# Attention over a 64x64 image: second key tiles in one-pass products, and a second chain of accumulating transfers for the denominators

## The chip, the cores and the metric

The kernel runs on one core of one Trainium2 chip, with its five engines: TensorE (PE in the profile), VectorE (DVE), ScalarE (ACT), GpSimd (POOL) and SyncE (SP), and its 16 DMA engines. The metric is the device time of one execution in microseconds, the median of several runs.

## The reference

Four images of 64x64 pixels with 256 channels pass through two layers. The first is attention over all 4096 pixels of an image, with queries and keys of 32 channels:

```python
q = x @ Wq + bq
k = x @ Wk + bk
v = x @ Wv + bv
energy = jnp.einsum('bnd,bmd->bnm', q, k)
attn = jax.nn.softmax(energy, axis=-1)
x_out = jnp.einsum('bnm,bmc->bnc', attn, v)
out = gamma * x_out.reshape(B, H, W, Cin) + inputs
```

The second layer is a 3x3 depthwise convolution to 768 channels, a product to 512, gelu, a product back to 256, added to its input, and then attention of each pixel to its 3x3 neighbours, added again. All is in float32.

## The kernel before, in words

**Slots.** An image is worked on in eight blocks of 512 query pixels, which makes 32 slots (slot s is block s % 8 of image s // 8). In a slot the 4096 keys pass in 16 half groups of two key tiles of 128, one at each of 16 points. The exponentials p of a half group are a tile of 128 keys by 2 x 512 queries. The convolution layer follows some slots behind: its pieces (hidden_part at L721, update L778, guide L874, local_values L941, scores L982, local_product L1075 and others) are jobs dealt out to the points of later slots, and its taps on VectorE (L608, L614) are dealt out by the list `share`, one number for each point.

**A point.** Program order is queue order on each engine, and at point n it is: loads on SP (keys ka and values v, a group of two half groups ahead); for a half group of IN_PARTS the high part of p(n+1) on ScalarE (high_part, L389); energy (L379 on TensorE, exponential L384 on ScalarE) for half group n+2; the send of p(n+1) where it is one of BY_DMA (L429, L431); the loads of forms of v (load_forms) for n+3; the jobs; the product of half group n (L403 or L415); add_up of n+1 on VectorE; the taps. Two PSUM banks hold one energy tile e, so the next energy waits for the exponential before. p has three buffers.

**Products.** A plain half group is four float32 matmuls (two key tiles, two halves of the channels; L403); each stands in the profile as two instructions of 128x512, so eight a half group. A half group of IN_PARTS (the even ones from 2 to 14) is written as three products in the one-pass type float32r: high of p with a mixed form of v, then low and gap of p with two other forms of v, 12 instructions (L415) into two pairs of accumulators, which finish adds up. Its price elsewhere: high on ScalarE, low (pl, L444) and gap (pg, L449) on VectorE, and the loads of the forms. Slots from 1 to 30 except 2 do so (in_two_sums); the others are plain throughout.

**Denominators.** den of a slot is the sum of its 16 p over the half groups. VectorE adds the even ones and 1 and 15 (L447). The odd ones from 3 to 13 go by DMA: GpSimd issues transfers of p into the tile sent, of which the first writes and the rest accumulate. At the end of add_up for 15, VectorE adds sent (L455) and folds the two halves (L456); partial_sums transposes and reduces (L474, L475) the denominators and the local sums; finish multiplies the parts by a matrix on TensorE (dps, L493), takes reciprocals (L496) and forms the output.

**Projections.** Slot 0 and the last slot of each image (7, 15, 23) compute queries, keys and values of the next image (project_qk, project_v, L317 to L355). project_v writes v of each pair of key tiles to DRAM: plain ones to packed_v, and the three forms of those in IN_PARTS to packed_f, from staging tiles of the tag "vs" with four buffers. The stores of the forms are issued by GpSimd.

**Slot 0 and 1.** In slot 0 weights are loaded and prepared: wup1 of the hidden layer at point 1, turn_weights at points 6 to 11. In slot 1 GpSimd prepares wmix (L653), between the sends.

Of the kernel before, what the change touches and what calls it, by code (L numbers as in the profile page):

```python
# [52 lines left out]
BY_DMA = (3, 5, 7, 9, 11, 13)  # L53
# [6 lines left out]
def attention_then_perception_kernel(  # L60
# [37 lines left out]
    def unshifted():  # L98
# [113 lines left out]
        packed_f = tc.dram_tile([P, NSLOT * 2, 3, 2 * C], F32, name="packed_f")  # L212
# [4 lines left out]
        def in_parts(s, G, half):  # L217
            return in_two_sums(s) and 2 * G + half in IN_PARTS

# [77 lines left out]
        def load_values(s, G):  # L297
            values[s, G] = tile_of([P, TPB, C], "v", f"v_{s}_{G}", 2)
            to = values[s, G].rearrange("p t c -> p (t c)")
            at = 2 * block(s, G)  # L300
            if not any(in_parts(s, G, half) for half in range(2)):
                nc.sync.dma_start(out=to, in_=packed_v[:, bass.ds(at * 2 * C, TPB * C)])
                return
            for half in range(2):
                if in_parts(s, G, half):
                    of = packed_f[:, at + half, 0]
                else:
                    of = packed_v[:, bass.ts(at + half, 2 * C)]
                nc.sync.dma_start(out=to[:, bass.ts(half, 2 * C)], in_=of)

        def load_forms(s, G, half):
# [3 lines left out]
                in_=packed_f[:, 2 * block(s, G) + half, 1:3],  # L315
# [5 lines left out]
        def project_v(s, pair, tag="m"):  # L321
# [10 lines left out]
            split = 2 * (s % NBLK) + pair in IN_PARTS  # L332
            if not split or s < NBLK or s >= NSLOT - NBLK:
# [10 lines left out]
                )  # L344
            if split:
                low, high = (fresh(f"v{n}_{s}_{pair}") for n in "lh")
                nc.scalar.copy(low, of)
                nc.scalar.activation(high.bitcast(F32R), of, AF.Identity, scale=BELOW)
                nc.vector.tensor_tensor(low, low, high, ALU.subtract)
                gap = fresh(f"vg_{s}_{pair}")  # L350
                nc.vector.scalar_tensor_tensor(gap, low, -SPLIT, high, ALU.mult, ALU.add)
                nc.vector.tensor_scalar(low, low, SPLIT, None, ALU.mult)
                for i, part in enumerate((high, low, gap)):
                    nc.gpsimd.dma_start(
                        out=packed_f[:, 2 * s + pair, i], in_=part.rearrange("p t c -> p (t c)")  # L355
                    )

        def projections(s):
            pair = [lambda: project_qk(s)] if s % 2 == 0 else []
            order = sorted(range(2), key=lambda n: 2 * (s % NBLK) + n in IN_PARTS)  # L360
            return [lambda n=n: project_v(s, n) for n in order] + pair
# [29 lines left out]

        def product(s, G, half):
# [7 lines left out]
            if not in_parts(s, G, half):  # L400
                for i in range(2):
                    for c in range(CH):
# [3 lines left out]
                        )  # L406
                return
# [14 lines left out]
        def by_dma(s, n):  # L422
            return 0 < s < NSLOT - 1 and n in BY_DMA

        def send(s, n):
            p = weights[s, n // 2, n % 2]
            if n == BY_DMA[0]:
                sent[s] = tile_of([P, 2, NB], "sent", f"sent_{s}")
                nc.gpsimd.dma_start(out=sent[s], in_=p)  # L429
            else:  # L430
                nc.gpsimd.dma_start(out=sent[s], in_=p, accum_op=ALU.add)  # L431

        def add_up(s, G, half):

            if by_dma(s, 2 * G + half):
                return
            p = weights[s, G, half]
            if G == 0 and half == 0:
                sums[s] = tile_of([P, 2, NB], "den", f"den_{s}")
                return  # L440
            if in_parts(s, G, half):
                high = highs[s, G, half]
                low, gap = (tile_of([P, 2, NB], f"p{n}", f"p{n}_{s}_{G}_{half}") for n in "lg")
                nc.vector.tensor_tensor(low.bitcast(F32R), p, high, ALU.subtract)  # L444
            den = sums[s]
            before = weights[s, 0, 0] if (G, half) == (0, 1) else den
            nc.vector.tensor_tensor(den, before, p, ALU.add)  # L447
# [5 lines left out]
            if G == NG - 1 and half == 1:  # L453
                if s in sent:
# [1283 lines left out]
```

## Time and profile before

| | before |
|---|---|
| median of 3 runs | 3292.66 us (3291.38 to 3293.06) |
| profiled execution, its own time | 3292.32 us |
| its span, first to last instruction | 3290.5 us |
| mean granted TensorE clock | 0.998 |
| busy: PE, DVE, ACT, POOL | 3263.0, 2728.5, 1349.2, 619.9 us |
| DMA: moved, mean rate | 505.29 MB, 154 GB/s |
| DMA queues, share of 16 engines | q1 (hardware) 35.6%, q0 (issued by GpSimd) 15.5% |

Where slot 12 stands in the span: from about 1028.9 to 1124.9 us, 96.0 us, like most slots. In this stretch PE is busy 96.00, DVE 84.45, ACT 40.59 and POOL 18.33 us, and the DMA share is 0.52. Slots 7, 15 and 23 take about 132 us.

How to read the lines. A line of a group has engine, operation, tiles out<-in, shape and count, then busy us and mean ns of one, then the idle time of the engine just before and what ended it. A line of a timeline has the start in us, the duration in us, engine, line of the code, operation, tiles, and in brackets the idle time before and its releaser; several alike in a row are one line with a count. The durations of matmuls include pipelining, so they overlap: what one costs is the distance from start to start. "Chain" is the work that ended last, followed back from the last instruction, as shares of the span.

### The profile page before, as it was taken

The page shows a single profiled execution, that of the slowest core. Times are in us where ns is not written, and L with a number is a line of the kernel's source. Part 1 is how long each engine was busy: PE and PEld are TensorE (multiplying, and loading weights), DVE is VectorE, ACT ScalarE, POOL GpSimd, SP SyncE. Part 2 cuts the span into 40 slices and gives each one's busy share as a digit, 9 for nine tenths or more (in the row PEclk, how much of TensorE's full clock was granted, in tenths as well). Part 3 has the DMA queues.
Part 4 walks back from the last instruction along what each step waited for, and adds up shares of the span by engine and source line. Part 5 has one row for each costly group of instructions (what it writes and reads, how often), then busy time and mean ns, then how long its engine had stood idle before and what let it go on. Part 6 is the DMA issues. An engine that isn't in the chain of part 4 may idle for free.

```text
span 3290.5 us, 35859 instructions
## 1 busy us (share of the span) xinstructions
PE 3263.0 (99%) x11986; PEld 2170.3 (66%) x11986; DVE 2728.5 (83%) x4093; ACT 1349.2 (41%) x1647; POOL 619.9 (19%) x807
## 2 busy tenths in 40 slices
PE   9999999999999999999999999999999999999998
PEld 5556667666666666676666666666666666666655
DVE  4678888878888888887888888887788888888894
ACT  3334444444444444444444444444444444444331
POOL 2201111121222221122112222211221122222021
PEclk9999999999999999999999999999999999999999
DMA  6655555575545554558554455546755544555100
GB/s 212 211 165 142 149 149 146 163 227 175 147 141 155 164 154 143 153 165 246 146 153 145 145 155 156 163 141 183 236 160 145 152 147 144 155 157 154 48 25 27
DMA packets 272831, 505.29 MB, mean 154 GB/s; under 512 B 95152, under 2 KB 96192, under 8 KB 272512
## 3 DMA queue, kind: packets, MB, share of 16 engines
q1 hardware_dynamic: 231632, 370.15, 35.6%
q0 software_dynamic: 33328, 119.33, 15.5%
q10 hardware_dynamic: 7680, 13.44, 1.1%
q8 instruction: 99, 1.62, 0.2%
q14 instruction: 92, 0.75, 0.1%
HBM read 346.92 MB, written 60.69 MB: 124 GB/s over the span
## 4 chain that ended last, share of the span: by engine, by line
PE 96%; DVE 1%; issue 1%; ACT 1%; DMA 1%; POOL 0%; SPq 0%; ACTq 0%; DVEq 0%; POOLq 0%
PE acc L403 32%; PE acc L415 17%; PE e L379 7%; PE dx L778 6%; PE hid_bc L721 5%; PE hid_gf L721 5%; PE hid_de L721 5%; PE lv L941 3%; PE g L874 3%; PE v L326 3%; PE lo L1075 3%; PE s L982 3%; PE hid_a L721 2%; DVE perc L608 1%; PE qk L260 1%; PE hid L753 1%
## 5 line engine op out<-in xcount | busy, mean ns | idle before, releaser
L403 PE MATMUL acc<-p,v 128*128 128x512 f32 x2472 | 1113.8, 593 | 0.2 <-ACT v L340 0.2
L608 DVE SCALAR_TENSOR_TENSOR perc<-xp,wb,perc 128x526 f32<-128x526 f32 (+1 forms) x1356 | 964.1, 771 | 1.4 <-ACT perc L604 1.3
L384 ACT ACTIVATE p<-e 128x1024 f32<-128x1024 f32 x512 | 524.2, 1024 | 1004.6 <-PE e L379 925.7
L403 PEld LDWEIGHTS acc<-p,v 128*128 128x128 f32 x2472 | 466.5, 190 | 486.7 <-issue 472.1
L379 PE MATMUL e<-qa,ka 128*128 128x512 f32 x1024 | 426.8, 498 | 7.6 <-DMA ka<-packed 4.3
L431 POOL DMA_DIRECT2D sent<-p x150 | 129.5, 864 | 1337.5 <-ACT p L384 1328.5
L447 DVE TENSOR_TENSOR den<-den,p 128x1024 f32<-128x1024 f32 x268 | 340.7, 1271 | 9.3 <-ACT p L384 9.1
L444 DVE TENSOR_TENSOR pl<-p,ph 128x1024 fp32r<-128x1024 f32 x203 | 248.3, 1223 | 66.4 <-ACT ph L389 66.2
L389 ACT ACTIVATE ph<-p 128x1024 fp32r<-128x1024 f32 x203 | 214.4, 1056 | 198.4 <-PE acc L415 124.2
L379 PEld LDWEIGHTS e<-qa,ka 128*128 128x128 f32 x1024 | 189.8, 189 | 155.9 <-issue 132.3
L415 PE MATMUL acc<-ph,v 128*128 128x512 f32 x812 | 264.7, 447 | 0.0
L449 DVE SCALAR_TENSOR_TENSOR pg<-pl,ph 128x1024 fp32r<-128x1024 f32 x203 | 257.9, 1271 | 0.0
L778 PE MATMUL dx<-hid,wup 128*128 128x512 f32 x512 | 229.8, 592 | 0.0
L415 PE MATMUL acc<-pl,vf 128*128 128x512 f32 x812 | 223.0, 396 | 0.0
L415 PE MATMUL acc<-pg,vf 128*128 128x512 f32 x812 | 219.1, 391 | 1.0 <-DVE pg L449 1.0
L1030 POOL TENSOR_TENSOR lsum<-lsum,lp 128x99 f32<-128x99 f32 (+1 forms) x179 | 197.3, 1109 | 11.7
L1007 POOL TENSOR_TENSOR lp<-lp,near 128x396 f32<-128x396 f32 x60 | 109.2, 1821 | 396.5 <-ACT lp L1002 396.5
L415 PEld LDWEIGHTS acc<-ph,v 128*128 128x128 f32 x812 | 148.2, 189 | 51.2 <-issue 23.0
L415 PEld LDWEIGHTS acc<-pl,vf 128*128 128x128 f32 x812 | 152.8, 188 | 37.1
L415 PEld LDWEIGHTS acc<-pg,vf 128*128 128x128 f32 x812 | 152.5, 188 | 37.4 <-DVE pg L449 1.5
L744 ACT ACTIVATE hid<-hid,bup 128x512 f32<-128x512 f32 x120 | 80.1, 715 | 215.4 <-DVE hid L728 215.4
L614 DVE TENSOR_TENSOR perc<-perc 128x262 f32<-128x262 f32 x360 | 155.8, 447 | 8.1
(206 smaller groups left out, 4021.5 us busy)
## 6 DMA issues: line engine op xcount, KB each, us to landing
vf<-packed_f SPq DMA_DIRECT2D x203, 512.0 KB, 3.8
sent<-p POOLq DMA_DIRECT2D x180, 512.0 KB, 5.2
ka<-packed SPq DMA_DIRECT2D x1016, 64.0 KB, 2.9
v<-packed_f SPq DMA_DIRECT2D x203, 256.0 KB, 2.7
v<-packed_v SPq DMA_DIRECT2D x203, 256.0 KB, 2.9
v<-packed_v SPq DMA_DIRECT2D x45, 512.0 KB, 3.4
xp<-in_x SPq DMA_DIRECT2D x30, 528.0 KB, 6.2
xc<-in_x SPq DMA_DIRECT2D x56, 256.0 KB, 4.7
```

Of the source, the lines that this page charges most:

```text
L379: nc.tensor.matmul(e[:, i, :], lhsT=keys[s, G][:, bass.ts(2 * half + i, P)].bitcast(F32R), rhs=queries[s].bitcast(F32R), start=True, stop= ...
L384: nc.scalar.activation(p, e, AF.Exp)
L389: nc.scalar.activation(high.bitcast(F32R), weights[s, G, half], AF.Identity, scale=BELOW)
L403: nc.tensor.matmul(accs[s][c], lhsT=v[:, i, bass.ts(c, P)], rhs=p[:, i, :], start=(first and i == 0), stop=(last and i == 1),)
L415: nc.tensor.matmul(accs[s][to + c], lhsT=w[:, i, bass.ts(c, P)].bitcast(F32R), rhs=x[:, i, :].bitcast(F32R), start=(to > 0 and n == 0 and ...
L444: nc.vector.tensor_tensor(low.bitcast(F32R), p, high, ALU.subtract)
L447: nc.vector.tensor_tensor(den, before, p, ALU.add)
L449: nc.vector.scalar_tensor_tensor(gap.bitcast(F32R), low, -SPLIT, high, ALU.mult, ALU.add)
L608: nc.vector.scalar_tensor_tensor(acc, win, wt, acc, ALU.mult, ALU.add)
L721: nc.tensor.matmul(ps[:, n * C : (n + 1) * C], lhsT=w(j), rhs=rows_of(mixes[s, j][:, kind, :]), start=(j == 0), stop=(j == MULT - 1),)
L778: nc.tensor.matmul(ps, lhsT=wup2[:, d, bass.ts(c, P)], rhs=hids[s][:, d, :], start=(d == 0), stop=(d == NHC - 1),)
L1030: nc.gpsimd.tensor_tensor(to, to, near_ws[block, half][:, t_, of, :], ALU.add)
```

## The change

In 26 slots (those in two sums, except the last block of each image) the six odd half groups 3 to 13 are no longer plain throughout: tile 0 keeps its two float32 matmuls (four instructions) and tile 1 is written as three one-pass products, six matmuls (six instructions). For this each of them gets a load of two forms (load_one, 256 KB), a high part on ScalarE (high_one), and low and gap on VectorE, all in the four buffers of "vs". In the same slots the denominators of half groups 4, 6, 8, 10 and 12 go by a second chain of accumulating transfers, in a buffer of the tag "xc", and VectorE adds two sent sums at the end.

The layout in DRAM follows: packed_h has v as the first product needs it (one load of 512 KB where there were two of 256), packed_f has the two other forms, packed_o those of single tiles. project_v makes the forms for single tiles too, and stores plain values a second time into packed_h. The pairs of a block are always projected in the order 1, 0. The list share deals the same 54 taps out otherwise. The load of wup1 in slot 0 goes from point 1 to point 4, and turn_weights from points 6 to 11 to points 8 to 13.

```diff
@@ -50,7 +50,8 @@
 IN_PARTS = (2, 4, 6, 8, 10, 12, 14)
-BY_DMA = (3, 5, 7, 9, 11, 13)
+ONE_IN_PARTS = (3, 5, 7, 9, 11, 13)
+BY_DMA = (ONE_IN_PARTS, (4, 6, 8, 10, 12))
@@ -209,13 +210,18 @@
         packed_v = tc.dram_tile([P, NSLOT * TPB * C], F32, name="packed_v")
-        packed_f = tc.dram_tile([P, NSLOT * 2, 3, 2 * C], F32, name="packed_f")
+        packed_h = tc.dram_tile([P, NSLOT, TPB * C], F32, name="packed_h")
+        packed_f = tc.dram_tile([P, NSLOT, 2, 2 * C], F32, name="packed_f")
+        packed_o = tc.dram_tile([P, NSLOT, 2, C], F32, name="packed_o")
...
             return in_two_sums(s) and 2 * G + half in IN_PARTS
+
+        def one_in_parts(s, n):
+            return in_two_sums(s) and s % NBLK < NBLK - 1 and n in ONE_IN_PARTS
@@ -297,22 +303,27 @@
             to = values[s, G].rearrange("p t c -> p (t c)")
-            at = 2 * block(s, G)
-            if not any(in_parts(s, G, half) for half in range(2)):
-                nc.sync.dma_start(out=to, in_=packed_v[:, bass.ds(at * 2 * C, TPB * C)])
-                return
-            for half in range(2):
-                if in_parts(s, G, half):
-                    of = packed_f[:, at + half, 0]
-                else:
-                    of = packed_v[:, bass.ts(at + half, 2 * C)]
-                nc.sync.dma_start(out=to[:, bass.ts(half, 2 * C)], in_=of)
+            at = block(s, G)
+            if not in_two_sums(s):
+                nc.sync.dma_start(out=to, in_=packed_v[:, bass.ts(at, TPB * C)])
+            elif s % NBLK < NBLK - 1:
+                nc.sync.dma_start(out=to, in_=packed_h[:, at])
+            else:
+                nc.sync.dma_start(out=to[:, : 2 * C], in_=packed_h[:, at, : 2 * C])
+                nc.sync.dma_start(out=to[:, 2 * C :], in_=packed_v[:, bass.ts(2 * at + 1, 2 * C)])
...
                 out=forms[s, G, half].rearrange("p (f t) c -> p f (t c)", f=2),
-                in_=packed_f[:, 2 * block(s, G) + half, 1:3],
+                in_=packed_f[:, block(s, G)],
+            )
+
+        def load_one(s, n):
+            forms[s, n] = tile_of([P, NB], "vs", f"vo_{s}_{n}", 4)
+            nc.sync.dma_start(
+                out=forms[s, n].rearrange("p (f c) -> p f c", c=C),
+                in_=packed_o[:, block(s, n // 2)],
             )
@@ -329,7 +340,9 @@
             of = ps.rearrange("p (t c) -> p t c", c=C)
-            split = 2 * (s % NBLK) + pair in IN_PARTS
+            n = 2 * (s % NBLK) + pair
+            split, one = n in IN_PARTS, n in ONE_IN_PARTS
+            h = packed_h[:, s, bass.ts(pair, 2 * C)].rearrange("p (t c) -> p t c", c=C)
             if not split or s < NBLK or s >= NSLOT - NBLK:
@@ -342,23 +355,30 @@
                 )
+                if not split:
+                    tiles = slice(0, 1 if one else 2)
+                    nc.gpsimd.dma_start(out=h[:, tiles], in_=v[:, tiles])
             if split:
-                low, high = (fresh(f"v{n}_{s}_{pair}") for n in "lh")
-                nc.scalar.copy(low, of)
-                nc.scalar.activation(high.bitcast(F32R), of, AF.Identity, scale=BELOW)
-                nc.vector.tensor_tensor(low, low, high, ALU.subtract)
-                gap = fresh(f"vg_{s}_{pair}")
-                nc.vector.scalar_tensor_tensor(gap, low, -SPLIT, high, ALU.mult, ALU.add)
-                nc.vector.tensor_scalar(low, low, SPLIT, None, ALU.mult)
-                for i, part in enumerate((high, low, gap)):
-                    nc.gpsimd.dma_start(
-                        out=packed_f[:, 2 * s + pair, i], in_=part.rearrange("p t c -> p (t c)")
-                    )
+                low, high, gap = (fresh(f"v{n}_{s}_{pair}") for n in "lhg")
+                to = h, packed_f[:, s, 0], packed_f[:, s, 1]
+            elif one:
+                both, gap = (fresh(f"v{n}_{s}_{pair}") for n in ("lh", "g"))
+                low, high, gap, of = both[:, 0:1], both[:, 1:2], gap[:, 0:1], of[:, 1:2]
+                to = h[:, 1:2], packed_o[:, s, 0], packed_o[:, s, 1]
+            else:
+                return
+            nc.scalar.copy(low, of)
+            nc.scalar.activation(high.bitcast(F32R), of, AF.Identity, scale=BELOW)
+            nc.vector.tensor_tensor(low, low, high, ALU.subtract)
+            nc.vector.scalar_tensor_tensor(gap, low, -SPLIT, high, ALU.mult, ALU.add)
+            nc.vector.tensor_scalar(low, low, SPLIT, None, ALU.mult)
+            nc.gpsimd.dma_start(out=to[0], in_=high)
+            for at, part in zip(to[1:], (low, gap)):
+                nc.gpsimd.dma_start(out=at, in_=part.rearrange("p t c -> p (t c)"))
...
             pair = [lambda: project_qk(s)] if s % 2 == 0 else []
-            order = sorted(range(2), key=lambda n: 2 * (s % NBLK) + n in IN_PARTS)
-            return [lambda n=n: project_v(s, n) for n in order] + pair
+            return [lambda: project_v(s, 1), lambda: project_v(s, 0)] + pair
@@ -389,6 +409,12 @@
+        def high_one(s, n):
+            high = tile_of([P, NB], "vs", f"oh_{s}_{n}", 4)
+            p = weights[s, n // 2, n % 2]
+            nc.scalar.activation(high.bitcast(F32R), p[:, 1, :], AF.Identity, scale=BELOW)
+            highs[s, n] = high
+
         def product(s, G, half):
@@ -398,12 +424,24 @@
             if not in_parts(s, G, half):
-                for i in range(2):
+                one = one_in_parts(s, 2 * G + half)
+                for i in range(1 if one else 2):
                     for c in range(CH):
...
                         )
+                if one:
+                    at = s, 2 * G + half
+                    f = forms.pop(at)
+                    for w, to, x in (
+                        (v[:, 1], 0, highs[at]), (f[:, :C], 0, lows[at]), (f[:, C:], CH, gaps[at])
+                    ):
+                        for c in range(CH):
+                            nc.tensor.matmul(
+                                accs[s][to + c], lhsT=w[:, bass.ts(c, P)].bitcast(F32R),
+                                rhs=x.bitcast(F32R), start=False, stop=False,
+                            )
                 return
@@ -420,39 +458,54 @@
         def by_dma(s, n):
-            return 0 < s < NSLOT - 1 and n in BY_DMA
+            if n in BY_DMA[1]:
+                return one_in_parts(s, ONE_IN_PARTS[0])
+            return 0 < s < NSLOT - 1 and n in BY_DMA[0]
...
             p = weights[s, n // 2, n % 2]
-            if n == BY_DMA[0]:
-                sent[s] = tile_of([P, 2, NB], "sent", f"sent_{s}")
-                nc.gpsimd.dma_start(out=sent[s], in_=p)
+            even = 1 - n % 2
+            if n == BY_DMA[even][0]:
+                tag, bufs = ("xc", 2) if even else ("sent", 1)
+                sent[s, even] = tile_of([P, 2, NB], tag, f"sent_{s}_{even}", bufs)
+                nc.gpsimd.dma_start(out=sent[s, even], in_=p)
             else:
-                nc.gpsimd.dma_start(out=sent[s], in_=p, accum_op=ALU.add)
+                nc.gpsimd.dma_start(out=sent[s, even], in_=p, accum_op=ALU.add)
...
-            if by_dma(s, 2 * G + half):
-                return
+            n = 2 * G + half
+            if one_in_parts(s, n):
+                low, gap = (tile_of([P, NB], "vs", f"o{x}_{s}_{n}", 4) for x in "lg")
+                high = highs[s, n]
+                nc.vector.tensor_tensor(
+                    low.bitcast(F32R), weights[s, G, half][:, 1, :], high, ALU.subtract
+                )
+                nc.vector.scalar_tensor_tensor(
+                    gap.bitcast(F32R), low, -SPLIT, high, ALU.mult, ALU.add
+                )
+                lows[s, n], gaps[s, n] = low, gap
             p = weights[s, G, half]
...
                 return
+            den = sums[s]
+            before = weights[s, 0, 0] if (G, half) == (0, 1) else den
             if in_parts(s, G, half):
                 high = highs[s, G, half]
-                low, gap = (tile_of([P, 2, NB], f"p{n}", f"p{n}_{s}_{G}_{half}") for n in "lg")
+                low, gap = (tile_of([P, 2, NB], f"p{x}", f"p{x}_{s}_{G}_{half}") for x in "lg")
                 nc.vector.tensor_tensor(low.bitcast(F32R), p, high, ALU.subtract)
-            den = sums[s]
-            before = weights[s, 0, 0] if (G, half) == (0, 1) else den
-            nc.vector.tensor_tensor(den, before, p, ALU.add)
+            if not by_dma(s, n):
+                nc.vector.tensor_tensor(den, before, p, ALU.add)
             if in_parts(s, G, half):
...
             if G == NG - 1 and half == 1:
-                if s in sent:
-                    nc.vector.tensor_tensor(den, den, sent.pop(s), ALU.add)
+                for even in range(2):
+                    if (s, even) in sent:
+                        nc.vector.tensor_tensor(den, den, sent.pop((s, even)), ALU.add)
                 nc.vector.tensor_tensor(den[:, 0, :], den[:, 0, :], den[:, 1, :], ALU.add)
@@ -1161,7 +1214,7 @@
-            share = [2, 4, 8, 6, 4, 1, 7, 3, 6, 3, 4, 2, 2, 1, 1, 0]
+            share = [1, 5, 8, 6, 5, 2, 7, 4, 6, 3, 4, 2, 1, 0, 0, 0]
             if slot == NSLOT - 1:
@@ -1187,6 +1240,8 @@
                 after = slot + (G + 1) // NG, (G + 1) % NG
+                if one_in_parts(slot, point + 1):
+                    load_one(slot, point + 1)
                 if half == 0:
@@ -1198,6 +1253,8 @@
                     high_part(*behind)
+                if one_in_parts(slot, point + 1):
+                    high_one(slot, point + 1)
                 if after[0] < NSLOT:
@@ -1233,8 +1290,6 @@
                     wperc, bperc = wb[:, :, :, :TAPS], wb[:, :, :, TAPS]
-                    wup1 = loaded(w_up1, "wup1", queue=nc.gpsimd)
-                    bup1 = loaded(b_up1, "bup1", queue=nc.gpsimd)
                     gam = loaded(gamma.partition_broadcast(P), "gam", [P, 1])
@@ -1245,8 +1300,11 @@
                     clear_tap(point - MULT)
-                if slot == 0 and 2 * MULT <= point < 4 * MULT:
-                    turn_weights(*divmod(point - 2 * MULT, 2))
+                if slot == 0 and point == NG // 2:
+                    wup1 = loaded(w_up1, "wup1", queue=nc.gpsimd)
+                    bup1 = loaded(b_up1, "bup1", queue=nc.gpsimd)
+                if slot == 0 and NG <= point < NG + 2 * MULT:
+                    turn_weights(*divmod(point - NG, 2))
                 if slot == 0 and point == NG:
```

## The prediction

> **What bounds the kernel now.** I read the page from the top: busy shares, then the chain of work that ended last, then the costliest groups.
>
> ```profile
> PE 3263.0 (99%) x11986; PEld 2170.3 (66%) x11986; DVE 2728.5 (83%) x4093; ACT 1349.2 (41%) x1647; POOL 619.9 (19%) x807
> PE 96%; DVE 1%; issue 1%; ACT 1%; DMA 1%; POOL 0%; SPq 0%; ACTq 0%; DVEq 0%; POOLq 0%
> L403 PE MATMUL acc<-p,v 128*128 128x512 f32 x2472 | 1113.8, 593 | 0.2 <-ACT v L340 0.2
> L415 PE MATMUL acc<-pl,vf 128*128 128x512 f32 x812 | 223.0, 396 | 0.0
> L447 DVE TENSOR_TENSOR den<-den,p 128x1024 f32<-128x1024 f32 x268 | 340.7, 1271 | 9.3 <-ACT p L384 9.1
> L431 POOL DMA_DIRECT2D sent<-p x150 | 129.5, 864 | 1337.5 <-ACT p L384 1328.5
> ```
>
> TensorE is the bound: it is busy 99% and makes 96% of the chain. Its whole idle time, by the list of waits, is some 17 us. So PE time taken away shows one for one, as long as nothing else becomes late. VectorE, at 83%, is the next.
>
> The mean durations overlap (matmuls are pipelined), so prices must be start to start. The timeline of TensorE in slot 12 gives them:
>
> ```profile
> 1056.10 3.60 PE L403 MATMUL acc<-p,v 128*128 128x512 f32 x8
> 1059.13 1.02 PE L379 MATMUL e<-qa,ka 128*128 128x512 f32 x2
> 1059.99 1.46 PE L721 MATMUL hid_a<-perc,wup 128*128 128x256 f32 x6
> ...
> 1131.12 1.10 PE L415 MATMUL acc<-pl,vf 128*128 128x512 f32 x4
> 1132.05 1.07 PE L415 MATMUL acc<-pg,vf 128*128 128x512 f32 x4
> 1132.96 0.61 PE L379 MATMUL e<-qa,ka 128*128 128x512 f32 x2
> 1133.42 3.59 PE L403 MATMUL acc<-p,v 128*128 128x512 f32 x8
> 1136.85 0.30 PE L493 MATMUL dps<-parts,fold 128*128 128x32 f32 x2
> ```
>
> Eight f32 instructions take 1133.42 to 1136.85, 3.43 us, so 0.429 each. Eight one-pass ones take 1131.12 to 1132.96, 1.84 us, so 0.230 each; over all I use 0.232. The first three lines test a change of form: 1056.10 to 1059.99 is 3.89 us, and 8 x 0.429 + 2 x 0.230 is 3.89. Passing from f32 to one-pass costs nothing beyond the two.
>
> **What the Trainium skill says.** TensorE: Matmul & The Clock Gate, section Back-to-back issue gap, gives 512/2.4 + 2.5 ns, about 216 ns, for an isolated 512-column matmul. The trace has 0.230 us for a one-pass instruction, 7% above, and 0.429 for an f32 one, twice 0.215. The same page, section HAM oscillation, says that PE idle gaps over about 3.4 us slow the clock afterwards. The trace has one such gap:
>
> ```profile
> 39.08 1.19 PE L379 MATMUL e<-qa,ka 128*128 128x512 f32 x2 [4.27 <-DMA ka<-packed]
> 40.07 5.39 PE L403 MATMUL acc<-p,v 128*128 128x512 f32 x8
> ```
>
> Eight matmuls took 5.39 us there and 3.59 elsewhere: a long stall costs some 2 us on top of itself. DMA: Bandwidth & Descriptors, section Anatomy of one DMA, puts a transfer issued by GpSimd at 2.0 us plus bytes/436e3. For 512 KB that is 3.2 us. The first, plain transfer of slot 12 landed in 3.06, but the accumulating ones have a median of 5.2, and I use that.
>
> **The change, part by part.**
>
> *Products.* 26 slots (1, 3 to 6, 8 to 14, 16 to 22, 24 to 30) have six mixed half groups, 156 in all. Each drops four f32 instructions (4 x 0.429 = 1.716) and adds six one-pass ones (6 x 0.232 = 1.392). That is -0.324 us each and **-50.5 us** in all, 1.94 us of a slot's 96.0. L403 should fall from x2472 to x1848.
>
> *VectorE per slot.* Low and gap of each mixed half group are twelve 128x512 operations, some 0.65 us each (the add over 512 columns, L456, is 0.67 from start to start). Five L447 adds go, at 1.14 each. One more add of the sent sum is 1.44. Together 7.8 - 5.7 + 1.44 = +3.5. The taps are the same 54, only dealt out otherwise. A steady slot has 84.45 us of VectorE in 96.0; it would have some 88 in 94.1, 93%. That still fits; what matters is where it falls. The end of a slot is tightest:
>
> ```profile
> 1124.88 1.22 DVE L444 TENSOR_TENSOR pl<-p,ph 128x1024 fp32r<-128x1024 f32 x1 [1.81 <-ACT ph L389]
> 1128.86 0.59 DVE L614 TENSOR_TENSOR perc<-perc 128x262 f32<-128x262 f32 x1
> 1130.81 1.49 DVE L455 TENSOR_TENSOR den<-den,sent 128x1024 f32<-128x1024 f32 x1
> 1133.00 0.47 DVE L614 TENSOR_TENSOR perc<-perc 128x262 f32<-128x262 f32 x1
> 1135.53 0.69 DVE L475 TENSOR_REDUCE parts<-turned 128x16 f32<-128x512 f32 x1
> ```
>
> VectorE runs without a gap from 1124.88 to 1136.22, and PE needs the parts at 1136.85 (dps): 0.63 us to spare. After the change this stretch gains 1.44 (second sent) and loses the two L614 (0.51 + 0.39, moved to earlier points), while PE comes 0.32 earlier. So 0.63 - 0.54 - 0.32 is -0.23; with the signal, PE waits about 0.3 us, 0 to 0.8. Behind dps stand the next energies, so this delays everything. Over 26 slots **+8 us** (0 to 21). Ahead of it the 1.81 us of idle at 1124.88 take up low and gap of point 13 and the 1.0 us by which PE comes earlier in points 9 to 13.
>
> *ScalarE.* Six 128x512 copies a slot, about 0.62 each (half of L389's 1056 ns and a little): 40.6 to some 44 us of 94. Hidden; were it not, 3.7 us a slot.
>
> *Second chain.* POOL issues five more sends a slot, 0.864 us each, 18.3 to 22.6 us. Buffers of p turn over by three: the exponential of n+3 waits for the landing of send n. In a steady slot that is three points, some 18 us, against 0.9 + 5.2. It costs nothing there, and still nothing at 10 us of landing.
>
> *Slot 1* is the exception. Its points are short, and POOL does the turning of weights (wmix) before it can send. The timelines of POOL and ScalarE:
>
> ```profile
> 157.49 0.92 POOL L431 DMA_DIRECT2D sent<-p  x1
> 167.45 0.89 POOL L431 DMA_DIRECT2D sent<-p  x1 [9.04 <-DMA sent<-p]
> ```
> ```profile
> 158.54 1.02 ACT L384 ACTIVATE p<-e 128x1024 f32<-128x1024 f32 x1 [0.57 <-PE e L379]
> 162.48 1.02 ACT L384 ACTIVATE p<-e 128x1024 f32<-128x1024 f32 x1 [2.92 <-PE e L379]
> 166.98 1.03 ACT L384 ACTIVATE p<-e 128x1024 f32<-128x1024 f32 x1 [2.38 <-DMA sent<-p]
> ```
>
> The send at 157.49, of half group 11, took 9.4 us to land, and the last exponential waited for it. Now the send of half group 10 stands there first, behind wmix too, and the exponential of 13 (158.54) needs its landing, some 8 us later. The next energies (161.37) wait for that exponential, since e has one buffer; 1.8 us are to spare. So PE stalls 6.2 us and loses 2 by the clock: **+8 us** once (3 to 12).
>
> *Loads.* +66 MB of sends and some 39 MB of loads on 505 MB; the DMA share of a steady slot rises from 0.52 to some 0.65. load_one stands on SP's queue a point ahead, waiting for the product two before: 3 us of landing against 6 us. Hidden.
>
> *Projections.* In slots 7, 15 and 23 (132 us each) every pair that was one plain form becomes three forms or a plain one with a second store. POOL's stores go from 21 to 48 an image, some 0.55 us each. The four buffers "vs" now wait for these stores: ScalarE's copies stand in its queue ahead of the exponentials, and wait. Mostly that is below 1 us and covered. At the seventh block POOL's sum of the local weights (L1030, 1.1 us an operation) stands ahead of the stores, and the exponential comes some 3 us late. I take 3.5 us a slot, **+10 us** for three (3 to 30). The profile before shows the like at a smaller size: PE waited for the copy vh three times, 2.5 us in all.
>
> *Slot 0.* The load of wup1 (1.5 MB, 9.3 us) goes from point 1 to point 4, away from the ka load that stalled PE 4.27 us at 39.08; a store by POOL now delays the prologue some 1.5 us. **-2 us** (-4 to +2).
>
> **Sum.** -50.5 + 8 + 8 + 10 - 2 = -26.5. The profiled execution took 3292.3 (its span 3290.5 and 1.8 around it), 0.3 under the median of the runs, 3292.66. 3292.3 - 26.5 is about **3266 us**.
>
> **Rivals.** (1) Everything is covered: -50.5 - 2, 3240 us. The steady slots speak for it (PE never waits in them); slot 1 speaks against. (2) VectorE takes a larger part: the new operations delay hid, guide or gaps in the middle of the slot, 1 us a slot in place of 0.3. Then 3266 + 18 = 3284. For it: from 1096.8 to 1123 VectorE has no gap at all; against it: it idles 7.8 us before 1097, waiting for PE. (3) Slower: VectorE becomes the bound of the steady slot. Its low and gap stand in line before the denominator, hidden-layer and guide work that PE waits for; the slot pays if VectorE's stretch between two waits for PE grows by more than it has to spare. The gain is gone from 1.94 us a slot on, less the 16 of the other terms: (50.5 - 16) / 26 = 1.3 us. At 2.5 us a slot: 3292.3 - 50.5 + 16 + 65 = 3323. (4) The change doesn't do what it says: one-pass instructions between f32 ones cost more. A penalty of 0.32 us a half group takes all, 3308 with the other terms. The sum of 3.89 above speaks against it.
>
> **How the numbers follow.** Chances: my sum 0.5, (1) 0.12, (2) 0.18, (3) 0.15, (4) 0.05. A change below 0.2% (6.6 us) can't be told from none here. Slower takes (3) and (4) but for a mild end of them, and some of a large stall in the projections: 0.17; within 0.2%: 0.07, from the upper end of (2); faster 0.76. The range is 3240 to 3298: from (1) to the mild end of (3), leaving out its worse half, part of (4) and a little below. The likeliest case alone has 3250 to 3280, from its terms' bounds.
>
> **What would show it.** Steady slots of 94.1 to 94.6 us in place of 96.0; L403 x1848 and one-pass groups at 0.23 from start to start; a wait of dps for parts of 0.3 us in most slots; one stall of 6 us near 160 us ended by an exponential that waited for a send; stalls in slots 7, 15 and 23 ended by exponentials. I am wrong if steady slots are above 95 us (VectorE), if mixed half groups take 3.4 us, or if exponentials wait for sends in steady slots.

## The result and the profile after

The changed kernel takes 3311.05 us (median of five runs, 3310.3 to 3315.98) against 3292.66 before (3291.38 to 3294.91): a ratio of 1.0058, with a 95% interval of 1.0044 to 1.0073. It is slower by 0.6%, where the prediction had 3266 us and faster. The profiled execution took 3311.05 us with a span of 3309.3; before it was 3290.5.

The page of the changed kernel, the parts that answer to those shown of before (busy shares, chain, groups):

```profile
PE 3234.4 (98%) x12298; PEld 2230.6 (67%) x12298; DVE 2860.0 (86%) x4373; ACT 1458.1 (44%) x1851; POOL 769.1 (23%) x1045
PE 70%; DVE 18%; issue 4%; DMA 4%; ACT 2%; POOL 1%; SPq 1%; ACTq 0%; DVEq 0%; POOLq 0%
L430 PE MATMUL acc<-p,v 128*128 128x512 f32 x1848 | 847.6, 594 | 0.2 <-ACT v L353 0.2
L399 PE MATMUL e<-qa,ka 128*128 128x512 f32 x1024 | 363.8, 436 | 25.9 <-ACT p L404 20.4
L473 POOL DMA_DIRECT2D sent<-p x254 | 218.6, 862 | 1126.7 <-ACT p L404 943.8
```

TensorE does less (3234 us in place of 3263), and L403, now L430, is at x1848 as forecast. But its share of the chain has gone from 96% to 70%, VectorE has 18%, and DMA 4%. TensorE now waits. Its list of waits:

```profile
PE e L399 <- ACT p L404: 20.4, 9, 4.5
PE dps L546 <- DVE parts L528: 9.1, 22, 0.9
PE c L978 <- ACT vh L371: 5.8, 3, 3.1
PE dx L831 <- ACT vh L371: 5.2, 3, 3.0
PE acc L453 <- DMA v<-packed_h: 5.1, 6, 1.9
```

The columns are total us, times, and the longest. In names, vs is the plain copy of a projected v, vh, vl and vg are the high part, low part and gap of a pair, vlh high and low of a single tile, and st the queries and keys. The dps line is the forecast wait at the end of a slot. The lines that name vh are not: TensorE waits for a copy that ScalarE makes for the projections.

Where the time went is read from the length of each slot, from one dps to the next (changes are to some 0.1 us):

| slots | before, us | after, us | change | forecast |
|---|---|---|---|---|
| 0 | 115.8 | 112.9 | -2.9 | -2 |
| 1 | 60.4 | 74.9 | +14.5 | -1.9 + 8 = +6 |
| 25 steady ones (3 to 6, 8 to 14, 16 to 22, 24 to 30) | mostly 96.0 | mostly 94.5 | -35.1 | 25 x (-1.94 + 0.3) = -41 |
| 7, 15, 23 | 132.0, 132.1, 134.3 | 143.3, 145.4, 153.2 | +43.5 | +10 |
| 2, 31, end | | | -1.1 | 0 |

The sum is +18.9, the spans' difference 18.8. The steady slots did nearly what was forecast. Two places took it back and more: slots 7, 15 and 23, in which the next image is projected, and slot 1.

**A steady slot.** TensorE's timeline at the end of slot 11 after:

```profile
1136.49 1.88 PE L430 MATMUL acc<-p,v 128*128 128x512 f32 x4
1137.80 1.03 PE L441 MATMUL acc<-oh,v 128*128 128x512 f32 x2
1138.67 0.63 PE L441 MATMUL acc<-ol,vo 128*128 128x512 f32 x2
1139.14 0.62 PE L441 MATMUL acc<-og,vo 128*128 128x512 f32 x2
1139.59 0.62 PE L399 MATMUL e<-qa,ka 128*128 128x512 f32 x2
...
1148.08 0.41 PE L546 MATMUL dps<-parts,fold 128*128 128x32 f32 x2 [0.77 <-DVE parts L528]
```

A mixed half group takes 1136.49 to 1139.59, 3.10 us (3.108 forecast), and dps waits for parts. The windows of slot 12 show VectorE at 87.73 of 94.53 us.

**A projection slot.** ScalarE in slot 7 after, then GpSimd and TensorE in the same stretch:

```profile
736.11 0.59 ACT L370 COPY vl<-v 128x512 f32<-128x512 f32 x1
741.39 0.60 ACT L371 ACTIVATE vh<-v 128x512 fp32r<-128x512 f32 x1 [4.70 <-DMA packed_h<-vs]
741.89 1.02 ACT L404 ACTIVATE p<-e 128x1024 f32<-128x1024 f32 x1
```
```profile
735.27 0.58 POOL L360 DMA_DIRECT2D packed_h<-vs  x1 [4.43 <-ACT vs L353]
743.18 0.54 POOL L375 DMA_DIRECT2D packed_h<-vh  x1 [4.48 <-ACT p L404]
```
```profile
742.96 0.73 PE L399 MATMUL e<-qa,ka 128*128 128x512 f32 x2 [1.84 <-ACT p L404]
743.53 3.60 PE L430 MATMUL acc<-p,v 128*128 128x512 f32 x8
...
755.33 0.20 PE L978 MATMUL c<-edge,ones 128*1 128x16 f32 x2 [2.08 <-ACT vh L371]
755.46 1.28 PE L453 MATMUL acc<-ph,v 128*128 128x512 f32 x4
756.54 1.91 PE L453 MATMUL acc<-pl,vf 128*128 128x512 f32 x4
```

The high copy vh takes the staging buffer of the plain copy vs, whose second store GpSimd issued at 735.27 and which gave the buffer back only at 741.4, 6 us later. ScalarE stands for 4.70 us, the exponential stands behind it, and TensorE's next energies behind that. The last line shows a second price: four matmuls take 1.91 us where 1.10 is usual.

**Slot 1.** GpSimd, ScalarE and TensorE after, then the windows (us, busy of PE, PEld, DVE, ACT and POOL, granted clock, DMA share, GB/s) of its last 58 us after and of its last 46 us before:

```profile
158.38 1.82 POOL L473 DMA_DIRECT2D sent<-p  x2
```
```profile
167.25 1.02 ACT L404 ACTIVATE p<-e 128x1024 f32<-128x1024 f32 x1 [6.02 <-DMA sent<-p]
```
```profile
168.32 0.73 PE L399 MATMUL e<-qa,ka 128*128 128x512 f32 x2 [1.64 <-ACT p L404]
```
```profile
130.00:187.80 57.80, 47.82 (x152) 31.29 (x150) 31.62 (x26) 20.43 (x23) 18.43 (x18) 0.88 0.94 251
```
```profile
130.00:176.20 46.20, 45.16 (x149) 27.55 (x147) 27.25 (x21) 18.58 (x19) 16.64 (x14) 1.00 0.91 251
```

The two sends behind wmix and the exponential that waits 6 us for the first of them are there as forecast. The DMA engines are 94% busy, but they were nearly so before (91%, the same 251 GB/s). New are a granted clock of 0.88 in place of 1.00, and TensorE's waits. In slot 1 after they are:

```profile
PE acc L453 <- DMA v<-packed_h: 4.7, 5, 1.9
PE e L399 <- DMA ka<-packed: 2.6, 2, 1.6
PE e L399 <- ACT p L404: 1.6, 1, 1.6
```

TensorE stands only 1.6 us for the exponential that waited 6, and 7.3 us for loads of v and of keys. Before, its one wait in this slot was 1.0 us, for pg.

### The profile page after: what moved, and what is told of

Read it like the earlier page. It is cut to its first block, busy times and chain, and to the rows that moved or that the text cites. A ratio compares the mean times of both kernels' runs of the same rounds, so it can differ in the third digit from the quotient of the medians.

```text
span 3309.3 us, 38174 instructions
## 1 busy us (share of the span) xinstructions
PE 3234.4 (98%) x12298; PEld 2230.6 (67%) x12298; DVE 2860.0 (86%) x4373; ACT 1458.1 (44%) x1851; POOL 769.1 (23%) x1045
## 4 chain that ended last, share of the span: by engine, by line
PE 70%; DVE 18%; issue 4%; DMA 4%; ACT 2%; POOL 1%; SPq 1%; ACTq 0%; DVEq 0%; POOLq 0%
PE acc L430 17%; PE acc L453 10%; PE dx L831 5%; PE e L399 5%; DVE perc L661 5%; PE hid_bc L774 5%; PE hid_de L774 4%; PE hid_gf L774 4%; PE acc L441 4%; PE lv L994 3%; PE g L927 2%; PE lo L1128 2%; PE hid_a L774 2%; DVE den L508 2%; DVE pl L497 2%
## 5 line engine op out<-in xcount | busy, mean ns | idle before, releaser
L661 DVE SCALAR_TENSOR_TENSOR perc<-xp,wb,perc 128x526 f32<-128x526 f32 (+1 forms) x1356 | 941.3, 759 | 2.2 <-ACT perc L657 2.0
L430 PE MATMUL acc<-p,v 128*128 128x512 f32 x1848 | 847.6, 594 | 0.2 <-ACT v L353 0.2
L430 PEld LDWEIGHTS acc<-p,v 128*128 128x128 f32 x1848 | 348.5, 190 | 338.5 <-issue 324.4
L473 POOL DMA_DIRECT2D sent<-p x254 | 218.6, 862 | 1126.7 <-ACT p L404 943.8
L399 PE MATMUL e<-qa,ka 128*128 128x512 f32 x1024 | 363.8, 436 | 25.9 <-ACT p L404 20.4
L501 DVE SCALAR_TENSOR_TENSOR pg<-pl,ph 128x1024 fp32r<-128x1024 f32 x203 | 265.5, 1308 | 8.8
L415 ACT ACTIVATE oh<-p 128x512 fp32r<-128x512 f32 x156 | 98.3, 630 | 324.5 <-PE acc L441 282.2
L1083 POOL TENSOR_TENSOR lsum<-lsum,lp 128x99 f32<-128x99 f32 (+1 forms) x179 | 211.9, 1191 | 11.7
L453 PEld LDWEIGHTS acc<-ph,v 128*128 128x128 f32 x812 | 149.4, 191 | 58.1 <-issue 26.8
L499 DVE TENSOR_TENSOR den<-den,p 128x1024 f32<-128x1024 f32 x138 | 183.5, 1330 | 5.6 <-ACT p L404 5.3
L667 DVE TENSOR_TENSOR perc<-perc 128x262 f32<-128x262 f32 x360 | 165.3, 480 | 6.3
```

The costliest lines, as they stand in the source:

```text
L399: nc.tensor.matmul(e[:, i, :], lhsT=keys[s, G][:, bass.ts(2 * half + i, P)].bitcast(F32R), rhs=queries[s].bitcast(F32R), start=True, stop= ...
L430: nc.tensor.matmul(accs[s][c], lhsT=v[:, i, bass.ts(c, P)], rhs=p[:, i, :], start=(first and i == 0), stop=(last and i == 1),)
L453: nc.tensor.matmul(accs[s][to + c], lhsT=w[:, i, bass.ts(c, P)].bitcast(F32R), rhs=x[:, i, :].bitcast(F32R), start=(to > 0 and n == 0 and ...
L473: nc.gpsimd.dma_start(out=sent[s, even], in_=p, accum_op=ALU.add)
L501: nc.vector.scalar_tensor_tensor(gap.bitcast(F32R), low, -SPLIT, high, ALU.mult, ALU.add)
L661: nc.vector.scalar_tensor_tensor(acc, win, wt, acc, ALU.mult, ALU.add)
```

## The experiments

The theory after the result: (T1) the projections' tiles turn over in too few staging buffers, copies wait for stores and exponentials stand behind them; (T2) in slot 1 the sends behind the turning of weights hold the exponentials. Against T1 stands the number of stores, on GpSimd's queue or on the DMA engines; against T2 the full DMA engines. A time without a range is that of one execution. Lines of the edits that are left out are marked by three dots.

**The layout alone.**

```diff
-            return in_two_sums(s) and s % NBLK < NBLK - 1 and n in ONE_IN_PARTS
+            return in_two_sums(s) and s % NBLK < NBLK - 1 and s < 0 and n in ONE_IN_PARTS
...
-            share = [1, 5, 8, 6, 5, 2, 7, 4, 6, 3, 4, 2, 1, 0, 0, 0]
+            share = [2, 4, 8, 6, 4, 1, 7, 3, 6, 3, 4, 2, 2, 1, 1, 0]
```

> The new layout and the projections that make it, with the products and denominators computed as before (no mixed half groups, no second chain, share as before). My theory (the projections' stores and their four staging buffers cost the three projection slots 43.5 us): slots 7, 15 and 23 stay near 143, 145 and 153 us, slot 1 goes back to some 60, steady slots to 96.0, the whole to some 3330 to 3336 us. Rival (the mixed products or sends lengthen the projection slots): they go back to 132 to 134 us and the whole to 3290 to 3295.

Measured: 3342.1 us. Slots 7, 15 and 23 take 146.8, 143.4 and 157.2; slot 1 takes 62.4, steady slots 96.0 to 96.1. With the products of before, the new projections alone cost 49 us. The change's gain in the steady slots is real; most of its price is here.

**The pairs of a block at two points.**

```diff
+                if nxt and slot and half == 0:
+                    nxt[G].pop(0)()
                 if nxt and half == 1:
```

> The changed kernel with the two pairs of a block projected at two successive points (pair 1 at the even, pair 0 at the odd), the same stores and copies. My theory (ScalarE's copies stand waiting for a staging buffer whose store was issued just before in the same point, and the exponentials stand behind them): slots 7, 15 and 23 fall from 143, 145, 153 to some 134 to 137 each, the whole by 20 to 30 us, to 3282 to 3291. Rival (the stores' number, on GpSimd's queue or on the DMA engines, is what costs): no change beyond 5 us, 3306 to 3316.

Measured: 3276.7 us, less than expected, and the three slots 134.9, 134.9 and 139.1. The same stores and copies, with time between them, cost 10 us in place of 43. The number of stores is out.

**Slot 1 as before, and both edits.**

```diff
-            return in_two_sums(s) and s % NBLK < NBLK - 1 and n in ONE_IN_PARTS
+            return in_two_sums(s) and s % NBLK < NBLK - 1 and s > 1 and n in ONE_IN_PARTS
...
```

> The changed kernel with slot 1 as before: no mixed half groups and no second chain in it. Both theories of slot 1 (DMA engines full; sends behind the weights' turning) expect slot 1 to fall from 74.9 to some 60 to 61 us and the whole by 13 to 15, to 3296 to 3298. If slot 1 stays above 68, it is the new loads in general (512 KB of v at once) or the moved load of wup1.

Measured: 3297.0 us, slot 1 at 61.1.

> Both of the last two edits. If they are separate causes, their gains add: 3267 to 3277 us, which is faster than both kernels. If the projections' cost is the number of stores: 3292 to 3302.

Measured: 3261.2 us, less than expected: the gains add (14 and 34 us apart, 50 together). More runs of this kernel stand below.

**Slot 1 in halves.** The first keeps its mixed half groups without the second chain, the other the second chain without mixed half groups. The edit of the first:

```diff
+        def second_chain(s):
+            return in_two_sums(s) and s % NBLK < NBLK - 1 and s > 1
...
             if n in BY_DMA[1]:
-                return one_in_parts(s, ONE_IN_PARTS[0])
+                return second_chain(s)
...
```

> The changed kernel with the mixed half groups in slot 1 but its denominators as before (no second chain there). As forecast on record, the stall of slot 1 is the sends behind the turning of weights: without the second chain slot 1 falls from 74.9 to some 61 us. Rival (the DMA engines are full in slot 1, 0.94 busy, and every load lands late): the traffic falls by five transfers of 512 KB of some 17 MB, and slot 1 falls only part of the way, to 64 to 70 us.

> The changed kernel with the second chain in slot 1 but its products as before (no mixed half groups there, so no loads of single forms). If the sends behind the turning of weights are the cause: slot 1 stays at 72 to 77 us. If the full DMA engines are: six loads of 256 KB of some 17 MB are gone, and slot 1 falls by some 3 to 6 us.

Measured: slot 1 takes 65.2 us with the mixed half groups alone and 74.7 with the chain alone, against 61.1 with neither and 74.9 with both. In eight other runs that leave slot 1 as in the changed kernel it took 71.4 to 77.1. TensorE's waits in slot 1 with the chain alone, and with the mixed half groups alone:

```profile
PE e L402 <- ACT p L407: 10.5, 3, 5.0
```
```profile
PE e L402 <- DMA ka<-packed: 2.4, 1, 2.4
PE acc L456 <- DMA v<-packed_h: 1.7, 2, 1.2
```

The chain is the cause that matters (13.6 us): exponentials wait for sends, and TensorE for them three times and not once. The loads come late where the mixed half groups are, and cost 4 us where the chain is not there. The two prices don't add: in the changed kernel, which has both, TensorE waits mostly for the loads and little for exponentials.

T2 holds in part only. With the chain alone, two of the three waits are for sends behind the turning of weights. The first is not: its send was issued at 140.57, and the turning begins at 145.24. GpSimd and ScalarE:

```profile
140.57 0.85 POOL L476 DMA_DIRECT2D sent<-p  x1 [4.57 <-ACT p L407]
...
145.24 2.35 POOL L709 TENSOR_TENSOR wmix<-wup 128x768 f32<-128x768 f32 x1
```
```profile
150.53 1.02 ACT L407 ACTIVATE p<-e 128x1024 f32<-128x1024 f32 x1 [8.26 <-DMA sent<-p]
```

That send took 9.9 us to land. The DMA engines were 82% busy over this slot and 83% over that of before, so the mean traffic doesn't explain it; what does, the two chains side by side or short peaks of traffic, was not tried apart. Whole times here (3309.1 and 3315.8) are not read: slots 7, 15 and 23 together took 7.1 and 2.5 us more than in the changed kernel, with the same instructions.

**No second chain at all.**

> The changed kernel without the second chain in any slot: VectorE adds the five denominators again. VectorE's work in a steady slot goes from 87.7 to some 92 us of 94.5. My theory: it becomes the bound, at the guides, gaps and the end of the slot, and steady slots go to 96 to 98 us, against some 4 us won in slot 1 or more; the whole 3320 to 3370. Rival (VectorE has room, the chain was not needed): steady slots 94.1 to 94.6 and the whole 3297 to 3303.

Measured: 3401.0 us, 31 more than the upper end expected. Steady slots mostly take 98.3 to 99.4, and VectorE has 92.2 of 98.5 us. TensorE's waits:

```profile
PE acc L456 <- DVE pg L504: 62.4, 51, 1.6
PE dps L549 <- DVE parts L531: 21.5, 24, 1.0
```

VectorE holds TensorE up although 6 us of the slot find it idle. The chain is worth some 4 us a slot; without it the mixed half groups lose to the 96.0 of before.

**The taps dealt out as before.**

> The changed kernel with the taps dealt out as before. My theory (the end of the slot is VectorE's chain up to dps; the two taps of points 13 and 14 stand in it): each steady slot grows by 0.6 to 0.9 us, the whole by 15 to 24, to 3326 to 3335. Rival (taps find room anywhere): within 4 us of 3311.

Measured: 3342.4 us, more than expected; steady slots mostly 95.7 to 97.9 in place of 94.4 to 95.2. The wait of dps for parts is 36.7 us in all, against 9.1. Dealing the taps out earlier is worth 1.3 us a slot, more than the 0.9 of the two taps that stood at its end. The new list also has up to three more taps done by the middle of the slot, and which of the two counts was not tried apart.

**Which buffer.** A tag is a ring of buffers, and the tag o has two. First only the plain copy goes there:

```diff
-                    v = fresh(f"vs_{s}_{pair}")
+                    v = tile_of([P, NB], "o", f"vs_{s}_{pair}", 2)
+                    v = v.rearrange("p (t c) -> p t c", c=C)
```

> The changed kernel with one thing moved: the plain copy of v in the projections of slots 7, 15 and 23 lies in a buffer of the tag o, which is idle then, in place of one of the four staging buffers. Stores, queues and program order stay. My theory (the high copy waits until the plain copy's stores have given its buffer back): that wait goes, the next to wait is the gap on VectorE or the pair of st; the three slots fall from 143, 145, 153 to some 134 to 140 and the whole to 3280 to 3296. Rival (the place in the point and the number of stores cost, not the buffers): 3306 to 3316.

Measured: 3311.8 us. A miss: the slots take 144.9, 144.0 and 149.4. ScalarE's waits around slot 7, in the changed kernel and then here:

```profile
ACT vh L371 <- DMA packed_h<-vs: 12.7, 5, 4.7
ACT st L277 <- DMA packed_o<-vg: 5.4, 2, 4.3
```
```profile
ACT st L277 <- DMA packed_o<-vg: 19.5, 3, 8.1
```

The wait of vh is gone, and st waits for the gap's store in its place.

> The changed kernel with the second store of the plain copy (into packed_h) issued by ScalarE, right behind the first, in place of GpSimd. If it is GpSimd's queue that brings this store late (behind sends and local sums), the three slots fall by 3 us or more each and the whole to 3295 to 3303. If it is the landing itself, some 3 to 6 us after the issue, little changes: 3304 to 3314.

Measured: 3312.4 us, the three slots 145.3, 147.9 and 154.1. ScalarE still waits 10.6 us for that store in slot 7, so GpSimd's queue is not what makes it late.

> The changed kernel with the pair st of the queries and keys in the tag o in place of the staging buffers; the plain copy stays in these. Theory, after the run with the plain copy moved alone changed nothing: two waits of ScalarE for buffers follow one another, and taking one away leaves the other. Here the waits of st for the gap's store should go (5 us in slot 7, more elsewhere) and those of the high copy for the plain copy's store stay (15 us in slot 7): the three slots fall by 0 to 5 us each, the whole 3296 to 3312.

```diff
-                tag, bufs = ("o", 2) if s < NBLK else ("vs", 4)
+                tag, bufs = ("o", 2)
```

Measured: 3311.5 us, with 146.7, 144.6 and 151.8; vh waits as before.

> Both in the tag o: the staging buffers then hold five tiles a block in place of six or eight, and st waits for the plain copy's stores, issued first, not for the gap's, issued last. If the buffers are the cause and not the place in the point or the number of stores: the three slots fall to 134 to 140 us and the whole to 3278 to 3296. If it stays at 3306 to 3316, the buffers are not the cause, and what remains is the work that stands ahead of the exponentials in the same point.

Measured: 3311.7 us. By its whole time this speaks against the buffers, as the expectation was written; by its slots it doesn't settle it. They take 140.6, 140.2 and 148.8, but slots 8, 16 and 24 take 102.2, 100.9 and 102.4 (96 to 97 in the changed kernel): finish needs a buffer of the tag o that still waits for a store. The wait in slot 7 has gone to VectorE:

```profile
DVE vg L374 <- DMA packed_o<-vlh: 20.2, 6, 5.5
```

Five tiles of a block in four buffers still make one wait. So a variant in which blocks 3 to 7 have four in four (the plain copy, but for the last block, and st in o as above, and):

```diff
-                low, high, gap = (fresh(f"v{n}_{s}_{pair}") for n in "lhg")
+                low, high = (fresh(f"v{n}_{s}_{pair}") for n in "lh")
+                if s >= NBLK and 2 <= s % NBLK < NBLK - 1:
+                    gap = tile_of([P, NB], "rden", f"vg_{s}_{pair}")
...
```

> The changed kernel with the pairs together, all stores kept, but for the third to seventh block of each projection the plain copy and st lie in the tag o and the gap of the whole pair in the tag rden, so that the four staging buffers hold exactly four tiles of a block (in the run before with copy and st in o they held five, and VectorE waited 20 us in slot 7 for the store of the first). If tiles over buffers are the cause: slot 7 falls from 143 to 133 to 137 us, slots 15 and 23 likewise, the whole to 3282 to 3296. If the work ahead of the exponentials in the same point is the cause, or the stores themselves: the whole stays at 3304 to 3316.

Measured: 3278.7 us, less than expected, slots 133.1, 133.5 and 143.6, and 96.3, 96.0 and 98.2 after them. VectorE's wait around slot 7:

```profile
DVE vg L380 <- DMA packed_o<-vlh: 3.1, 1, 3.1
```

With order, stores and operations unchanged, buffers alone bring slots 7 and 15 to within 1.5 us of before. In slot 23 the whole pairs are also stored in plain form, which is one more tile a block, the likely reason that it keeps 9 us. This settles T1 for the other two.

> The changed kernel with the pairs together, but from the second image on the forms of single tiles are left out (their two copies on ScalarE, three operations on VectorE and three stores a block); the products read those of the first image in their place, with the same loads, and the plain copy is still stored a second time. Staging tiles a block are then four or six, as before the change. If the forms of single tiles make the cost (by their tiles, copies and stores): slots 7, 15 and 23 fall to 132 to 137 us, the whole to 3270 to 3290. If it is the second store of the plain copy: they stay above 139, the whole above 3300.

Measured: 3272.2 us, slots 132.7, 133.1 and 136.4. The second store of the plain copy alone costs some 2 us a slot at most; the forms of single tiles, with their two tiles a block, make the cost.

**The version that beats both.** It has slot 1 as before and the pairs at two points. It, and then the same with a tap dealt out earlier and with the plain copy in the tag o:

> The kernel with slot 1 as before and the pairs projected apart, timed: 3259 to 3264 us, a ratio of 0.990 to 0.991 to before.

Measured: 3262.21 us (3261.49 to 3264.06, five runs) against 3290.94 (nine runs of before on that chip): a ratio of 0.9916, 95% interval 0.9902 to 0.9929.

> The same, and the one tap of point 12 dealt to point 1, where VectorE still waits for TensorE. If the end of the slot is what VectorE's work sets, dps comes earlier by up to the tap (0.7 us) as far as it waited (0.25 to 0.85 us): 6 to 12 us less, 3250 to 3256. If VectorE is behind by its total since the second point, the same.

Measured: 3263.76 us, 0.9921 (0.9908 to 0.9935), a miss: the same. Slots 10 and 11 won 0.1 to 0.2 us, slots 3 and 4 lost 0.4 to 0.9, and most did not change.

> Slot 1 as before, pairs projected apart, and the plain copy in the tag o. The waits for buffers left in slots 7, 15 and 23 (2 to 5 us each) should shrink: 3252 to 3262 us. If the wait only moves to another tile, as it did before: 3259 to 3266.

Measured: 3272.48 us, 0.9946 (0.9929 to 0.9963), a miss of 10 us: slots 7, 15 and 23 take 137.5, 137.3 and 142.3. TensorE now waits 9.3 us in three times for lo of VectorE (L1145) ahead of qk; that these copies in the tag o hold up lo, which lies in the same tag, is the likely reading and was not tried apart.

## Why the prediction was wrong

The forecast was -26.5 us, and the spans differ by +18.8, which is 45.3 us more. By its own steps:

- *Products, -50.5.* Right: x1848, 3.10 us a mixed half group, nothing for the passage between forms.
- *VectorE per slot, +8.* Right in place, 6 us too small. In 25 slots the sum is -35.1, so 13.4 us were given back where 7.5 was forecast for these slots (25 x 0.3): 0.54 a slot. dps waits for parts, some 0.25 us in most slots and 0.77 to 0.85 at the end of slots such as 10 and 11, 9.1 us in all; the rest was not traced.
- *ScalarE and loads hidden, the second chain free in a steady slot.* Right in the steady slots: none shows an exponential that waits for a send, and TensorE waits for a load of v once, 0.4 us. The DMA share came to 0.72 in slot 12, not 0.65. In slot 1 loads were not hidden.
- *Slot 1, +8.* Half the size, and a part of the path was missing. The change is +14.5, or +16.4 beside the 1.9 it should have won. The forecast wait is there on ScalarE (6.0 us), but the step let it pass to TensorE whole, 6.2 us and 2 of clock. TensorE was late by then and stood 1.6 us for it. Of its 10 us of waits 7.3 are for loads, which the step had not priced in this slot, and the granted clock of 0.91 over the slot costs some 7 us more (an estimate, 0.09 of 74.9). Where the chain stands alone, TensorE does wait for exponentials, 10.5 us, and at three sends where the step had one. Sends take 3.9 to 12.2 us to land in this slot, against 3.4 to 9.4 before.
- *Projections, +10.* This step failed. It named the right buffers and the engine whose queue stands, and then took 3.5 us a slot from one exponential at the seventh block, where GpSimd's sums stand ahead of the stores. Measured: 11.3, 13.3 and 18.9. With six or eight tiles a block in four buffers, the fifth tile (vh) waits for the store of the block's own plain copy, the sixth (vg) for that of vlh, and in blocks with queries and keys st waits too. In slot 7 this came to 12.7 us on ScalarE before vh, 5.4 before st, and 10.1 on VectorE before vg. The step should have counted tiles a block against buffers: before, four tiles (plain, three forms) or six, after, six or eight. About 30 of the 43.5 us are idle TensorE. The rest is matmuls that take longer, most of it by a granted clock of 0.99, 0.99 and 0.97 in the three slots, for which the step had nothing.
- *The like in the profile before.* The three waits for vh, 2.5 us, that the step took for a smaller case of this were none. They stand just behind slots 7, 15 and 23, and the changed kernel has them unchanged:

```profile
PE hid_a L774 <- ACT vh L371: 2.5, 3, 1.6
```

- *Slot 0, -2.* It came out at -2.9; TensorE's wait for a ka load, 4.27 us before, is 0.7 after. It was not tried apart.

The rivals: the one that ended on the slower side was VectorE as the bound of a steady slot. It did not happen; but the run without the second chain shows how near it was (98.5 us), and the run with the old taps too. The slower result came from two places that the forecast had both in its sum, together at a third of their size. The upper ends that it gave them, 12 and 30 us, were also too low.

## What to carry to other kernels

Where a change gives a short stage more tiles, count the tiles of one step against the buffers of their ring: each tile over it can wait for a transfer's landing, on whatever engine writes that tile, and moving one tile away here only handed the wait to the next. Spreading the steps over time (the three slots 10 us above before) did as much as buffers enough for most blocks (12 us), and takes no memory. And read a short stage by itself: loads that are hidden in a steady slot made most of TensorE's waits in slot 1.

## What the runs showed of the hardware

Stalls of some 2 us were followed by a lowered clock. In slot 7 after, TensorE's longest stalls were 1.84 us, ahead of the energies at 742.96, and 2.08 us, ahead of 755.33. The eight matmuls behind the first took their usual 3.60 us. Behind the second the granted clock was half for 3.41 us; the columns are as above:

```profile
753.03:756.44 3.41, 1.33 (x7) 0.93 (x7) 1.09 (x2) 0.62 (x2) 2.35 (x5) 1.00 0.38 154
756.44:759.85 3.41, 3.41 (x9) 2.62 (x9) 1.92 (x4) 2.40 (x4) 1.16 (x3) 0.50 0.69 274
```

The same followed two shorter stalls in a row. In slot 1 these were 1.57 and 0.67 us:

```profile
135.21:138.62 3.41, 1.17 (x5) 0.34 (x4) 1.38 (x2) 1.27 (x2) 0.00 (x0) 1.00 1.03 270
138.62:142.03 3.41, 3.41 (x8) 2.73 (x9) 0.00 (x0) 1.44 (x2) 0.85 (x1) 0.50 1.02 255
```

The Trainium skill, TensorE: Matmul & The Clock Gate, section HAM oscillation, speaks of gaps over about 3.4 us. Here one gap of 2.08 us was enough, and so were two of 2.24 together, so in this trace the measurement decides: TensorE was idle for more than half of the 3.41 us ahead of each drop shown. Where exactly the border lies was not tried.
